# The order of Pool's work around the scan's next keys, and layer 0's norm as fused DVE operations

## The chip, the cores and the metric

The kernel runs on one core of one Trainium2 chip. A core has five engines with a queue of instructions each, worked through in order: TensorE (PE, matrix multiplies into PSUM), VectorE (DVE), ScalarE (ACT), GpSimd (POOL in the profile, Pool here) and SyncE (SP, which in this kernel issues nearly all the DMA transfers). An instruction starts when those ahead of it on its engine have started or ended and when the semaphores that it waits for have been raised by other engines or by DMA transfers. The metric is the device time of one execution in microseconds, as the median of several runs: 3565.93 us before the change (3 runs, 3565.69 to 3568.84).

## The reference, cut to what matters

The input is x of 16 batches, 512 tokens, 128 channels. Two layers follow each other, and each adds two branches to x:

```
xn = layernorm(x)
x  = x + memory(xn) + block0(xn)          # layer 0
xn = layernorm(x)
x  = x + attention1(xn) + experts1(xn)    # layer 1
```

The memory branch of layer 0 is a recurrence. The 512 tokens are cut into 8 chunks of 64; for each chunk c, the keys are k = rmsnorm(silu(xn wk)) * k_norm and the values v = silu(xn wv); a two-layer network with weights w0, w1 and a gain ln is trained by one gradient step on (k, v) of all 16 batches, the gradient is clipped by its norm, and momentum and decay give the next weights. Chunk c+1 needs the weights of chunk c. After chunk 7 the trained network is read out with queries for all tokens.

block0 is a convolution, an attention with 16 heads of 8 channels over 512 tokens, a residual, a layer norm with gain g and shift b, and eight experts of width 512 that all tokens go through, weighted by a softmax gate:

```
x  = conv(xn)
x  = layernorm(x + attention(x) @ wo.T + bo, g1, b1)     # "the norm behind layer 0's attention"
x  = layernorm(x + sum_e probs[e] * (relu(x @ w1[e] + b1[e]) @ w2[e] + b2[e]), g2, b2)
```

Layer 1 has two causal attentions with a convolution between them, and 32 experts of which each token goes to 8.

## The kernel before, in words

Everything is cut by batch into [128 partitions, 4 token tiles, 128 channels]. Each piece of work is a Python generator that writes a few instructions and then yields. A driver (`Turns.run`, line 284) goes through all live generators once per turn in the order of their priorities; a turn is one row of heads of attention scores, so that every turn holds some attention, some expert matmuls and a share of whatever else is live. `idle(n)` lets n turns pass; `room()` waits in turns for a free PSUM bank; `mark` and `after` pass word from one generator to another in turns. There are 1275 turns.

Only PE keeps the order in which the generators wrote its instructions (`manual_schedule(engines=ORDERED)`, lines 651 and 691). For DVE, ACT, Pool and SP a scheduler places each instruction on its engine's queue: by its own reckoning of when the operands are ready, and among those that are ready by the order of writing, with `high_priority` ones ahead. So a yield moves PE's instructions by a turn, and those of the other engines only as far as the scheduler lets it.

What is live in layer 0, by stage:

- Attention of batch b, every 32 turns: `front0` projects q, k, v; `tops` and `largest` (line 379) compute scores on PE and their row maximum on DVE (L404, `nm<-s`); `weighted` computes the scores again the other way round, ACT takes the exponential (L476), PE multiplies with the values; `post0` (line 1131) finishes the batch.
- `post0`: output projection on PE (`po`), bias on DVE (L1148), then `layernorm` (line 230): `moments` gives mean and variance by DVE (L222, L223) and 1/sqrt(variance + eps) by two small Pool operations (`rsqrt`, L213 and L214). Then four Pool operations normalise a token tile each (L237), one Pool operation over 128x512 multiplies by the gain (L243) and one adds the shift (L245). Four idle turns later SP stores x1 (L1153), PE transposes it, and SP stores the transposed copy (L1157). There are 16 `post0`.
- `ffn` (line 547): the eight experts of a batch, in pieces that fill the turns; after each expert Pool adds its output to a sum (L619, `ac<-ac,y`).
- `scan` (line 786): steps c = 0 to 7, 42 turns each. In a step, `hidden` computes the network's hidden layer and its slope (Pool: L891, L892), `gradient(0)` and `gradient(1)` the gradient of the output for half the tokens each. Each starts with a copy and four squares with row sums on ACT (L914, L266), the `rsqrt` of them on Pool (`r_y`), and then a multiply on DVE (L920) that waits for it. At the end of a step the clip factor `cl` goes from PE to ACT to two Pool operations (L1004, L1005) to DVE (L1007), and DVE updates the weights (L1010 to L1015).
- `project(c + 2)` is started at the end of step c: it projects keys and values of the chunk after next, squares the keys on ACT (eight L266 `sq<-k`), takes their `rsqrt` on Pool (`r_k`) and then does three Pool operations over 128x1024 each: `k<-k,sb_rowsA` (L836), `k<-k,r_k` (L838), `v<-k,v` (L840). They are called the key operations below.
- `readout` (line 1024), every six turns after the scan, 16 times: a query's projection, `rsqrt` and two Pool operations (L1034, L1035), the hidden layer (`ppq` on PE, L1047 and L1048 on ACT, L1050 on DVE into `hTq`), the output (`pyq` on PE, which reads `hTq`), `rsqrt`, one DVE operation (L1065), three Pool operations (L1066 to L1068) and a store by SP (L1070).

Layer 1 begins in turns while layer 0's last batches are still at work; it is the same before and after the change, apart from where the scheduler and the pace of the experts put its pieces.

Of the kernel before, what the change touches and what calls it, by code (L numbers as in the profile page):

```python
# [14 lines left out]
ALU = mybir.AluOpType  # L15
# [5 lines left out]
TB = S // P  # L21
# [52 lines left out]
def bc(ap, axis, n):  # L74

    u = ap.unsqueeze(axis)
    shape = list(u.shape)
    shape[axis] = n
    return u.to_broadcast(shape)
# [3 lines left out]
def network(ctx: ExitStack, tc: tile.TileContext, a, out):  # L83
    nc = tc.nc
# [30 lines left out]
    def load_rows(pool, name, names):  # L115
        t = pool.tile([P, len(names) * D], F32, bufs=1, name="sb_" + name)
        nc.sync.dma_start(t, a[name].partition_broadcast(P))
        return {n: t[:, i * D : (i + 1) * D] for i, n in enumerate(names)}
# [15 lines left out]
    row = load_rows(const, "rowsC", ["gb"])  # L134
# [28 lines left out]
    def room():  # L163

        while held[0] >= pools["work"]:
            yield
# [16 lines left out]
    def flat(ap):  # L183
        return ap.rearrange("p t d -> p (t d)")
# [24 lines left out]
    def rsqrt(dst, src, scale, eps, n):  # L209

        with tc.high_priority():
            t = sm.tile([P, n], F32, tag="rs_t", name="rs_t")
            nc.gpsimd.tensor_scalar(t, src, scale, eps, ALU.mult, ALU.add)  # L213
            nc.gpsimd.tensor_tensor(dst, t, nhalf[:, :n], ALU.pow)  # L214

    def moments(src, out):

        st = sm.tile([P, TB, 6], F32, tag="ln_st", name="ln_st")
        mv = sm.tile([P, TB, 2], F32, tag="ln_mv", name="ln_mv")
        rs = sm.tile([P, TB], F32, tag="ln_rs", name="ln_rs")  # L220
        for t in range(TB):
            nc.vector.bn_stats(st[:, t, :], src[:, t, :])  # L222
            nc.vector.bn_aggr(mv[:, t, :], st[:, t, :])  # L223
            if t == 1:
                yield
        rsqrt(rs, mv[:, :, 1], 1.0, 1e-5, TB)
        out.append((mv, rs))
        yield

    def layernorm(dst, src, gain=None, shift=None, on=None):  # L230


        got = []
        yield from moments(src, got)
        mv, rs = got[0]
        for t in range(TB):
            (on or (nc.gpsimd,))[t % len(on or (0,))].tensor_scalar(  # L237
                dst[:, t, :], src[:, t, :], mv[:, t, 0:1], rs[:, t : t + 1], ALU.subtract, ALU.mult
            )
            if t % 2 == 1:  # L240
                yield
        if gain is not None:
            nc.gpsimd.tensor_tensor(dst, dst, bc(gain, 1, TB), ALU.mult)  # L243
            yield
            nc.gpsimd.tensor_tensor(dst, dst, bc(shift, 1, TB), ALU.add)  # L245
            yield
# [26 lines left out]
    def idle(n):  # L273
        for _ in range(n):
            yield
# [493 lines left out]
    def side(*parts):  # L769

        going, parts = [], list(parts)
        while parts or going:
            if parts:
                going.append(parts.pop(0))
            going = [g for g in going if next(g, StopIteration) is not StopIteration]
            yield
# [9 lines left out]
    def scan(s1):  # L786
# [13 lines left out]
        def tokens_of(c):  # L800
            xc = s1.tile([P, B, CHUNK], F32, tag="gy", name="xc")
            nc.sync.dma_start(xc, xt[0].rearrange("b p (c t) -> c p b t", t=CHUNK)[c])
            return xc.rearrange("p b t -> p (b t)")
# [13 lines left out]
        def project(c):  # L817

            xc = tokens_of(c)
            yield from idle(3)  # L820
            k = s1.tile([P, NT, D], F32, tag="k", bufs=2, name="k")
            v = s1.tile([P, NT, D], F32, tag="v", bufs=2, name="v")

            def half(dst, w, q):
                return silu_half(
                    flat(dst[:, 4 * q : 4 * q + 4, :]),
                    lambda t: xc[:, (4 * q + t) * P : (4 * q + t + 1) * P], A(w),
                )

            yield from side(half(k, "wk", 0), half(k, "wk", 1), half(v, "wv", 0), half(v, "wv", 1))  # L830
            ks[c] = k, v
            mark("read", c)
            rk = sm.tile([P, NT], F32, tag="r_k", name="r_k")
            rms_rows(rk, k, NT, s1)
            yield
            nc.gpsimd.tensor_tensor(k, k, bc(row["kn"], 1, NT), ALU.mult)  # L836
            yield
            nc.gpsimd.tensor_tensor(k, k, bc(rk, 2, D), ALU.mult)  # L838
            yield
            nc.gpsimd.tensor_tensor(v, k, v, ALU.subtract)  # L840
            yield from idle(2)
            mark("keys", c)
# [181 lines left out]
        def readout(b):  # L1024
            xb = s1.tile([P, TB, D], F32, tag=("k", "v")[b % 2], bufs=2, name="xb")
            nc.sync.dma_start(xb, x_b[b])
            xT = s1.tile([P, S], F32, tag=("hT0", "kT")[b % 2], name="xTr")
            nc.sync.dma_start(xT, xt[0, b])
            yield from idle(2)
            q = s1.tile([P, TB, D], F32, tag=("yh", "eb", "gy", "hT1")[b % 4], name="rq")  # L1030
            yield from silu_half(flat(q), lambda t: xT[:, t * P : (t + 1) * P], A("wq"))
            rq = sm.tile([P, TB], F32, tag="r_q", name="r_q")
            rms_rows(rq, q, TB, s1)
            nc.gpsimd.tensor_tensor(q, q, bc(row["qn"], 1, TB), ALU.mult)  # L1034
            nc.gpsimd.tensor_tensor(q, q, bc(rq, 2, D), ALU.mult)  # L1035
            yield from idle(5)
            yield from room()
            qT = s1.tile([P, S], F32, tag="sg", bufs=2, name="qT")
            transpose_tokens(qT, q)
            yield from idle(1)  # L1040
            hT = s1.tile([P, 2, S], F32, tag=("h", "ds")[b % 2], name="hTq")

            def hidden(i):
                yield from room()
                pp = hold("ppq")
                mm(pp, w0T[:, i * P : (i + 1) * P], qT)
                nc.scalar.activation(hT[:, i, :], pp, AF.Tanh, scale=0.5)  # L1047
                nc.scalar.activation(hT[:, i, :], hT[:, i, :], AF.Copy, scale=0.5, bias=0.5)  # L1048
                yield
                nc.vector.tensor_tensor(hT[:, i, :], hT[:, i, :], pp, ALU.mult)  # L1050
                drop()
                yield

            yield from side(hidden(0), hidden(1))
            yield from room()
            py = toks(work("pyq"))
            for t in range(TB):
                for i in range(2):
                    mm(py[:, t, :], hT[:, i, t * P : (t + 1) * P], w1T[:, i, :], start=(i == 0), stop=(i == 1))
            ry = sm.tile([P, TB], F32, tag="r_yq", name="r_yq")  # L1060
            y = s1.tile([P, TB, D], F32, tag=("h", "ds")[b % 2], name="yq")
            nc.scalar.copy(y, py)
            rms_rows(ry, y, TB, s1)
            yield from idle(3)
            nc.vector.tensor_tensor(y, y, bc(ry, 2, D), ALU.mult)  # L1065
            nc.gpsimd.tensor_tensor(y, y, bc(ln, 1, TB), ALU.mult)  # L1066
            nc.gpsimd.tensor_tensor(y, y, q, ALU.add)
            nc.gpsimd.tensor_tensor(y, y, xb, ALU.add)  # L1068
            yield from idle(3)
            nc.sync.dma_start(acc_b[b], y)  # L1070
            yield
# [59 lines left out]
    def post0(b):  # L1131
        yield from after(("back", 0, b, 0, 0), ("back", 0, b, 0, 1))
        z = live.pop((0, b))
        xcT, cn = z["xcT"], z["cn"]
        free_values.append(z["vp"])
        yield from room()
        cT = fa.tile([P, S], F32, tag="st", bufs=2, name="cT")
        transpose_tokens(cT, cn)
        yield from idle(2)
        yield from room()  # L1140
        po = toks(hold("po"))
        for t in range(TB):
            tk = slice(t * P, (t + 1) * P)
            mm(po[:, t, :], cT[:, tk], Wt("wo"), stop=False)
            mm(po[:, t, :], xcT[:, tk], ident, start=False)
        x1 = fa.tile([P, TB, D], F32, tag="x1", bufs=1, name="x1")
        yield
        nc.vector.tensor_tensor(x1, po, bc(row["bo0"], 1, TB), ALU.add)  # L1148
        drop()
        yield  # L1150
        yield from layernorm(x1, x1, row["g1"], row["b1n"])
        yield from idle(4)
        nc.sync.dma_start(x1d[0, b], flat(x1))  # L1153
        yield from room()
        x1T = fa.tile([P, S], F32, tag="st", bufs=2, name="x1T")
        transpose_tokens(x1T, x1)
        nc.sync.dma_start(x1d[1, b], x1T)  # L1157
        mark("x1", b)
        yield
# [494 lines left out]
```

## Time and profile before

| | before |
|---|---|
| median of the runs | 3565.93 us (3565.69 to 3568.84) |
| the profiled execution's own time | 3557.66 us |
| its span, first to last instruction | 3555.9 us |
| PE busy | 3379.7 us, 95% |
| DVE busy | 2315.6 us, 65% |
| ACT busy | 2233.4 us, 63% |
| Pool busy | 1508.2 us, 42% |
| mean granted TensorE clock | 0.975 |

The profiled execution is 8.3 us, or 0.23%, faster than the median of the runs. By stage, from the table of windows: the scan's steps lie between about 130 and 1140 us, the readouts between 1140 and 1500 us, the last three `post0` of layer 0 end at about 1700 us, and what follows is layer 1 alone.

| window, us | PE idle, us | DVE busy | Pool busy |
|---|---|---|---|
| 130 to 1140 | 36.3 | 66% | 35% |
| 1140 to 1500 | 14.7 | 60% | 49% |
| 1500 to 1700 | 6.0 | 60% | 35% |
| 1700 to 3556 | 85.4 | 67% | 46% |

How to read such a table: PE works in a fixed order and is busy nearly all the time, so the time is PE's work and the gaps in it. Idle time of another engine costs nothing in itself; it counts where an instruction of PE ends up waiting for it. A second thing to read is the granted clock: after some gaps the clock stands at half for a few microseconds, and PE's work takes longer there.

### The profile page before, as it was taken

Reading aid. Unit: us, or ns where it says so; the run is one execution under the profiler, and the core shown is the slowest. Engines: PE = TensorE matmul, PEld = TensorE weight load, DVE = VectorE, ACT = ScalarE, POOL = GpSimd, SP = SyncE. Lnnn points to the kernel's source line nnn. Section 1 sums busy time; section 2 is a strip of 40 time slices with the busy share of each in tenths; the row PEclk is TensorE's granted clock in tenths of the full one; section 3 lists DMA queues with packets and bytes.
Section 4 is the critical chain, followed back from the end, with each engine's and each line's share of the span. In section 5 each row is a group of like instructions: output and inputs, shape, how many; then the busy total and the mean of one; then the engine's idle time right before and its main releaser. Section 6 shows DMA issues by size and latency. Waiting matters only on the chain.

```text
span 3555.9 us, 63951 instructions
## 1 busy us (share of the span) xinstructions
PE 3379.7 (95%) x22085; PEld 1897.3 (53%) x22085; DVE 2315.6 (65%) x6045; ACT 2233.4 (63%) x4951; POOL 1508.2 (42%) x2354
## 2 busy tenths in 40 slices
PE   6999999999999999999999999999999999998887
PEld 3445555554555555455555565555555555554443
DVE  5676666656766566556467667666666666567875
ACT  1566766775766787666656666665666666664444
POOL 5323432432431455432544344443444344433654
PEclk7999999999999999999999999999999999998998
DMA  5222222222122332443434443444344443433343
GB/s 178 70 71 77 71 82 74 74 77 83 56 85 86 102 109 87 133 122 102 135 108 122 124 125 115 130 126 121 107 122 122 124 125 98 134 106 98 93 102 93
DMA packets 289794, 370.37 MB, mean 104 GB/s; under 512 B 45984, under 2 KB 141376, under 8 KB 289088
## 3 DMA queue, kind: packets, MB, share of 16 engines
q1 hardware_dynamic: 282304, 359.46, 35.0%
q0 software_dynamic: 7168, 6.82, 1.2%
q8 instruction: 177, 2.90, 0.3%
q14 instruction: 145, 1.19, 0.1%
HBM read 236.58 MB, written 132.99 MB: 104 GB/s over the span
## 4 chain that ended last, share of the span: by engine, by line
PE 50%; DVE 5%; DMA 3%; ACT 1%; POOL 1%; issue 1%; SPq 1%; POOLq 0%; DVEq 0%; ACTq 0%
PE s L197 13%; PE pye L611 10%; PE phe L197 10%; PE pc L197 9%; PE pq L197 1%; DVE s L396 1%; PE fill L206 1%; DVE nm L404 1%; PE tpc L252 1%; PE tp L252 1%; DVE s L403 1%; PE po L197 1%; ACT e L476 1%; DMA rq<-lo 1%; PE pv L197 1%
## 5 line engine op out<-in xcount | busy, mean ns | idle before, releaser
L476 ACT ACTIVATE e<-s 128x512 f32<-128x512 f32 (+1 forms) x2432 | 1278.3, 577 | 556.4 <-PE s L197 517.2
L404 DVE TENSOR_REDUCE nm<-s 128x1 f32<-128x512 f32 (+2 forms) x1408 | 907.5, 682 | 510.1 <-PE s L197 509.2
L396 DVE CUSTOM_DVE_ANT_0 s<-s,sb_const 128x512 f32<-128x512 f32 (+1 forms) x1024 | 623.4, 643 | 390.3 <-PE s L197 388.9
L484 POOL TENSOR_SCALAR_AFFINE_SELECT e<-e 128x128 f32<-128x128 f32 (+2 forms) x1270 | 429.6, 347 | 751.0 <-ACT e L476 726.5
L197 PE MATMUL s<-kx,qx 64*128 64x512 f32 (+3 forms) x3072 | 620.4, 429 | 26.8 <-DMA kx<-rk 13.5
L197 PE MATMUL pc<-e,vp 128*32 128x512 f32 (+3 forms) x6144 | 621.7, 502 | 13.9 <-POOL e L484 7.8
L611 PEld LDWEIGHTS pye<-ew,hTe 128*128 128x128 f32 x4096 | 519.0, 192 | 178.7 <-issue 157.9
L197 PEld LDWEIGHTS s<-kx,qx 64*128 64x128 f32 x3072 | 271.2, 187 | 555.2 <-issue 219.4
L611 PE MATMUL pye<-ew,hTe 128*128 128x128 f32 x4096 | 562.3, 281 | 1.5 <-ACT hTe L601 1.4
L197 PE MATMUL s<-qx,kx 64*128 64x512 f32 (+3 forms) x3072 | 535.7, 356 | 27.2 <-DVE nm L404 8.4
L197 PE MATMUL phe<-x1T,ew 128*128 128x512 f32 x1024 | 551.1, 623 | 7.8 <-DMA ew<-in_ew 3.1
L601 ACT ACTIVATE hTe<-phe,sb_cols 128x512 f32<-128x512 f32 x512 | 354.1, 692 | 245.2 <-PE phe L197 242.8
L197 PEld LDWEIGHTS s<-qx,kx 64*128 64x128 f32 x3072 | 305.5, 188 | 80.4 <-ACT e L476 19.1
L619 POOL TENSOR_TENSOR ac<-ac,y 128x512 f32<-128x512 f32 x128 | 163.9, 1280 | 425.9 <-ACT y L618 363.9
L403 DVE TENSOR_TENSOR s<-s,sb_const 128x256 f32<-128x256 f32 (+1 forms) x384 | 181.6, 515 | 190.5 <-PE s L197 157.4
L197 PEld LDWEIGHTS pc<-e,vp 128*32 128x32 f32 x6144 | 151.4, 110 | 238.1 <-issue 173.2
L197 PEld LDWEIGHTS phe<-x1T,ew 128*128 128x128 f32 x1024 | 158.8, 193 | 75.0 <-issue 44.1
L618 ACT ACTIVATE y<-pye,pr 128x128 f32<-128x128 f32 x512 | 147.5, 370 | 30.6 <-PE pye L611 26.2
L396 DVE DVE_READ_ACCUMULATOR2_ANT nm<- 128x1 f32 x1024 | 144.1, 141 | 0.0
L213 POOL TENSOR_SCALAR rs_t<-ss 128x4 f32<-128x4 f32 (+1 forms) x56 | 12.0, 215 | 221.5 <-ACT sq L266 220.0
L1470 POOL DMA_INDIRECT acc<-eo,sidx x32 | 52.0, 1624 | 72.2 <-DVE eo L1464 26.3
L213 POOL TENSOR_SCALAR rs_t<-ln_mv 128x4 f32<-128x4 f32 x64 | 12.8, 200 | 162.3 <-DVE ln_mv L223 159.4
(302 smaller groups left out, 3906.4 us busy)
## 6 DMA issues: line engine op xcount, KB each, us to landing
ew<-in_ew SPq DMA_DIRECT2D x256, 256.0 KB
kx<-rk SPq DMA_DIRECT2D x192, 256.0 KB
qx<-rq SPq DMA_DIRECT2D x128, 256.0 KB
rq<-hi SPq DMA_DIRECT2D x64, 256.0 KB
rq<-lo SPq DMA_DIRECT2D x64, 256.0 KB
rk<-hi SPq DMA_DIRECT2D x64, 256.0 KB
rk<-lo SPq DMA_DIRECT2D x64, 256.0 KB
qx<-r SPq DMA_DIRECT2D x64, 256.0 KB
```

The source lines that it names most:

```text
L197: nc.tensor.matmul(o, lhsT=lhsT, rhs=rhs, start=start, stop=stop)
L252: nc.tensor.transpose(tp[:, t * P : (t + 1) * P], src(t), ident)
L396: newest[0] = nc.vector.tensor_tensor_reduce(out=sv[r][:, 0, :], in0=sv[r][:, 0, :], in1=row["caus"][:, S - n :], scale=1.0, scalar=-BIG, ...
L403: nc.vector.tensor_tensor(dg, dg, bc(row["caus"][:, S - P :], 1, per), ALU.add)
L404: newest[0] = nc.vector.tensor_reduce(nm[:, qt, r, t : t + per], sv[r], AX.X, ALU.max)
L476: nc.scalar.activation(e[:, r, 0 : per * n], s[r], AF.Exp, scale=SCALE)
L484: cleared[0] = nc.gpsimd.affine_select(out=ev[:, r, :, 0:P], in_=ev[:, r, :, 0:P], pattern=[[0, per], [1, P]], compare_op=ALU.is_ge, fill= ...
L601: nc.scalar.activation(hs[i], ph, AF.Relu, bias=col("fb", i))
L611: nc.tensor.matmul(pye[0][:, t, :], lhsT=h[:, t * P : (t + 1) * P], rhs=w2[e][:, f, :], start=(f == 0 and t == 0), stop=(f == 3), skip_gro ...
L618: nc.scalar.mul(y[:, t, :], pye[0][:, t, :], pr[:, t, e : e + 1])
L619: nc.gpsimd.tensor_tensor(ac, ac, y, ALU.add)
L1470: nc.gpsimd.indirect_dma_start(out=acc, out_offset=bass.IndirectOffsetOnAxis(ap=sidx[:, e : e + 1], axis=0), in_=eo[:, i, :], in_offset=No ...
```

## The change

Three places are edited.

- In `project`, one yield between the squares of the keys and the key operations becomes nine idle turns, except for chunks 0 and 1.
- In `readout`, one more idle turn stands between the hidden layer and the output's matmuls `pyq`.
- In `post0`, the call of `layernorm` is replaced: `moments` stays, with its small Pool `rsqrt`; then four DVE operations compute (x - mean) * gain for a token tile each, and four more compute that times 1/sqrt(variance + eps), plus the shift. Two are written per turn. The wait before the store is two turns in place of four.

```diff
@@ project(c)
             rms_rows(rk, k, NT, s1)
-            yield
+            yield from idle(9 if c > 1 else 1)
             nc.gpsimd.tensor_tensor(k, k, bc(row["kn"], 1, NT), ALU.mult)
             yield
             nc.gpsimd.tensor_tensor(k, k, bc(rk, 2, D), ALU.mult)
@@ readout(b)
             yield from side(hidden(0), hidden(1))
+            yield from idle(1)
             yield from room()
             py = toks(work("pyq"))
@@ post0(b)
-        yield from layernorm(x1, x1, row["g1"], row["b1n"])
-        yield from idle(4)
+        got = []
+        yield from moments(x1, got)
+        mv, rs = got[0]
+        for t in range(TB):
+            nc.vector.scalar_tensor_tensor(
+                x1[:, t, :], x1[:, t, :], mv[:, t, 0:1], row["g1"], ALU.subtract, ALU.mult
+            )
+            if t % 2 == 1:
+                yield
+        for t in range(TB):
+            nc.vector.scalar_tensor_tensor(
+                x1[:, t, :], x1[:, t, :], rs[:, t : t + 1], row["b1n"], ALU.mult, ALU.add
+            )
+            if t % 2 == 1:
+                yield
+        yield from idle(2)
         nc.sync.dma_start(x1d[0, b], flat(x1))
```

The two new groups of DVE operations are at lines 1156 and 1162 of the changed kernel; lines behind them are 15 higher than before.

## The prediction

> **What bounds the kernel now.** I read the page first: PE is busy 95% of the span. Then the table of windows by stage. The change lies between 130 and 1580 us, and there PE is idle 51.6 us, of which 36.3 fall in the scan's steps and 14.7 in the readouts (columns: window, length, PE busy, weight loads, DVE, ACT, Pool, granted clock, DMA):
>
> ```profile
> 130.00:1140.00 1010.00, 973.66 (x5713) 537.50 (x5705) 666.22 (x1226) 680.18 (x1558) 354.96 (x335) 0.99 0.26 74
> 1140.00:1500.00 360.00, 345.35 (x2036) 183.90 (x2035) 215.52 (x384) 275.53 (x712) 177.77 (x183) 0.99 0.36 107
> ```
>
> So nothing but a gap of PE can be won, and half clock behind a gap. Third, the waits from 130 to 1600 us (total, times, longest): PE waits most for the row maxima of DVE, and DVE in turn for two small Pool results.
>
> ```profile
> PE s L197 <- DVE nm L404: 15.5, 14, 4.2
> ...
> DVE yh L920 <- POOL r_y L214: 23.5, 6, 9.9
> ...
> DVE cl L1007 <- POOL cl L1005: 4.5, 1, 4.5
> ```
>
> Fourth, the timelines of these places. At the end of scan step 3, the norm behind the attention stands on Pool ahead of the clip factor; DVE stands at L1007 with the maxima behind it, and PE stops:
>
> ```profile
> 622.05 3.15 POOL L237 TENSOR_SCALAR x<-x,ln_mv,ln_rs 128x128 f32<-128x128 f32 x4
> ...
> 626.39 1.28 POOL L243 TENSOR_TENSOR x<-x,sb_rows 128x512 f32<-128x512 f32 x1
> 627.75 1.26 POOL L245 TENSOR_TENSOR x<-x,sb_rows 128x512 f32<-128x512 f32 x1
> ...
> 629.89 0.16 DVE L1007 RECIPROCAL cl<-cl 128x1 f32<-128x1 f32 x1 [4.47 <-POOL cl L1005]
> ...
> 631.95 0.49 PE L197 MATMUL s<-kx,qx 64*128 64x512 f32 x1 [3.34 <-DVE nm L404]
> ```
>
> In step 5 the key operations of the next chunk stand on Pool ahead of the second gradient's `r_y`:
>
> ```profile
> 792.88 2.73 POOL L836 TENSOR_TENSOR k<-k,sb_rowsA 128x1024 f32<-128x1024 f32 x1
> ...
> 799.25 2.34 POOL L840 TENSOR_TENSOR v<-k,v 128x1024 f32<-128x1024 f32 x1
> ...
> 801.96 1.01 POOL L214 TENSOR_TENSOR r_y<-rs_t,nhalf 128x4 f32<-128x4 f32 x1
> ...
> 803.00 0.69 DVE L920 TENSOR_TENSOR yh<-yh,r_y 128x512 f32<-128x512 f32 x1 [6.28 <-POOL r_y L214]
> ...
> 804.34 0.79 PE L197 MATMUL s<-kx,qx 64*128 64x512 f32 x2 [4.23 <-DVE nm L404]
> ```
>
> And three gaps in the readouts, with the clock behind the second and third (eighth column):
>
> ```profile
> 1228.39 1.13 PE L197 MATMUL ppq<-qT,sb_pa 128*128 128x512 f32 x2 [2.02 <-ACT hTe L601]
> ...
> 1343.51 2.80 PE L197 MATMUL pyq<-sb_pa,hTq 128*128 128x128 f32 x11 [3.05 <-DVE hTq L1050]
> ...
> 1425.09 1.65 PE L197 MATMUL pgt<-sb_gw,x1T 128*128 128x8 f32 x8 [1.70 <-DMA x1T<-x1d]
> ...
> 1343.00:1347.00 4.00, 3.49 (x17) 3.48 (x18) 0.96 (x2) 0.65 (x2) 0.00 (x0) 0.57 0.50 151
> 1425.00:1433.00 8.00, 7.91 (x32) 3.44 (x34) 2.36 (x6) 3.53 (x12) 1.01 (x1) 0.57 0.77 220
> ```
>
> A clock of 0.57 over 4 us is 0.43 x 4 = 1.7 us of PE work lost; over 8 us it is 3.4. The window from 633 to 637 us shows 0.57 too.
>
> **The nine turns.** They do nothing. Built with this edit alone, the program has on all five engines the instruction order of the kernel before. The scheduler places Pool's work by when operands are ready, and the key operations follow their squares. In the changed kernel they still stand between the first and the second `r_y` in steps 2, 3, 5 and 6. Price 0, and the 6.28 us stall of step 5 stays.
>
> **The norm taken off Pool.** Each of 16 `post0` loses six Pool operations: 3.15 + 1.28 + 1.26 = 5.7 us, 91 us in all. Pool is not the bound, so I count only the places where something waits behind them.
>
> (a) Step 3's clip factor. In the new Pool order only the norm's `rsqrt` (done at 621.94) and one L619 (1.27 us) precede it, its operand is there at 622.3, and the pair takes 0.9 us: done at about 624.2 against 629.9, before DVE asks in earnest. The gap of 3.34 and the 1.7 of clock go: -5.0.
>
> (b) The gap at 1425. SP stood at the store L1153 from 1404 to 1414 us for L245, then at the readout's store L1070 until 1421.6 for Pool operations that had queued behind the norm; the load of x1T came after both. Without the norm (6.2 us there) and with the readout one turn later (six turns are 18.9 us, so 3.15) the load is issued 3 us earlier, more than the 1.70 that PE waited. -1.7 - 3.4 = -5.1.
>
> (c) The gap at 1228 and 0.66 us at 1218.8 (PE waits for `rq` of L1035). Both follow a norm on Pool, 1208.6 to 1215.0: L1034 and L1068 come behind it, and ACT's L1047, which starts at 1226.5, writes the buffer that readout 1's store, issued only at 1223.96, still reads. 6.4 us earlier and one turn later is 3.2 earlier, more than the 2.02: -2.7.
>
> **The readout's idle turn.** At 1343 `pyq` followed `hTq` at once; a turn of 3.15 us just covers 3.05: -3.05 - 1.7 = -4.75. The cost: the store of one readout comes a turn nearer to the write of the buffer by the readout after next. The tightest pairs apart from (c) lie 5.9 and 6.2 us apart from issue to write, and a store takes some 2.5 us; 3.15 more fits. 0.
>
> **What the change puts in the way.** (d) In step 4 the key operations ran before both `r_y` (650.98 to 660.51 us) and nobody waited. In the new Pool order they stand between the two, as in the other steps. There the second `r_y` ends 14.4 to 15.6 us after the first; in step 4 that is 682.0 to 683.2, and DVE comes to its multiply at 677.47: a new stall of 4.5 to 5.7 us. What PE pays for such a stall the four other steps show: 9.90 us of stall cost 1.1 (gap at 436.8), 3.63 cost 2.7 (546.7 to 555.4), 1.18 cost 5.0 (929.6 to 945.1 with one half-clock stretch), 6.28 cost 12.6 (gaps of 4.23, 1.15, 1.38 and 0.69, clock 1.7 + 3.4). The mean is 5.4; less 0.4 that step 4 lost already, +5.0, with ends 0.7 and 12.2.
>
> (e) In steps 2 and 5 an L619 now stands between the sum of squares and the second `r_y`: 1.27 us on top of both stalls. Ends 0 (step 2's 9.90 hardly cost anything) and 2.5 (once for once): +2.5, since step 5 passed most of its stall on.
>
> (f) DVE gets 128 operations. The nearest row is L1011, the same kind at 128x128: it starts at 630.95 and the next at 631.21, so 0.26 us each, 33 us. Each reads two SBUF operands, and such operations are stretched while Pool works: L1065 has a mean of 975 ns against 679 undisturbed, the eight groups of 16 from L920 to L942 average 744 against some 675. I take 0.1 us each, 13 us. These 46 us go into DVE's idle time (344 us in the scan's window), but four groups stand among the maxima, and the second pair waits for Pool's `rsqrt`, with the maxima of that turn queued behind it and PE behind those. Ends: 0, and all 46 on PE. From 130 to 1580 us DVE is busy 927 us, 622 of them in L404; the other 305 cost PE the 15.5 us of waits for L404, 5%. By that rate 46 us cost +2.3.
>
> [...]
>
> SP's two stores of x1 come two turns earlier; what waited behind L1153 on SP waited 87 us over ten times, and only (b) reached PE. The work left on PE is the same but for 512 columns of filler.
>
> **The sum.** (a) to (c) and the readout's turn: -5.0 - 5.1 - 2.7 - 4.75 = -17.55; with (d) to (f) -17.55 + 5.0 + 2.5 + 2.3 = -7.75. The profiled execution would go from 3557.66 to 3549.9; it lies 8.3 below the median of the runs, so the median goes from 3565.9 to 3558.
>
> **Rivals.** First, nothing measurable: step 4 pays like step 5, 12.2 in place of 5.0, and the sum is -0.6: 3565.3. For it: the same engines and the same pattern; against it: two of the four steps paid under 3. Second, slower: DVE becomes what PE waits for. The place is the four groups in front of L404 in each `post0`; from 17 of their 46 us on PE, 15 more than my 2.3, the change is slower by 7; at half, 23, the sum is +13: 3579. For it: 14 waits for L404 already, and DVE two thirds busy; against it: most DVE idle time before L404 (477 us) is spent waiting for PE. Third, more gain: step 4 pays as little as step 2, 0.7, and the sum is -12.1: 3553.9. Fourth, the nine turns do after all what they say: then the 1.1 + 2.7 + 12.6 + 5.0 = 21.4 of the four steps go, with (d) and (e): -17.55 - 21.4 + 2.3 = -36.7: 3529. The instruction order speaks against it.
>
> **Numbers.** About 0.2%, 7.1 us, is what a measurement of this kernel can tell from no change. Forecast 0.33, third rival 0.10, fourth 0.02: faster 0.45. First rival, and cases between: same 0.31. Second: slower 0.24. The forecast's own range is 3551 to 3559. The whole range reaches down to (d) and (f) at their low ends with some gap more (3546), up to near the second rival (3577).
>
> **What would show it.** Right: no gap of 3 us before 632; no SP wait for Pool at L1153; `pyq` without a wait for `hTq`; a new DVE wait for `r_y` in step 4 of about 5 us, and those of steps 2, 3 and 5 still there. Wrong: key operations behind the second `r_y`; PE's wait for L404 far above 15 us in the window to 1600; new gaps in layer 1, where the pieces of the experts shift and 91 us of PE idle time after 1500 could move either way.

## The result, and the profile after

The changed kernel is slower: 3576.13 us in the median of 13 runs against 3565.69 us in 13 runs of the kernel before on the same chip, a ratio of 1.0024 with a 95% interval of 1.0014 to 1.0034, or some 9 us. The prediction had said 3558, and faster.

The profiled execution of the changed kernel took 3576.36 us, at its median. That of the kernel before took 3557.66, some 8 us below its own. So the two profiles lie 18.7 us apart, of which some 10 are only the difference between two executions. The first experiment below has the instruction order of the kernel before on all five engines and was profiled at 3563.34 us; it serves as a second profile of that order.

The table of windows by stage of the changed kernel (columns as in the prediction):

```profile
130.00:1140.00 1010.00, 964.58 (x5657) 536.22 (x5653) 682.19 (x1291) 672.37 (x1542) 294.49 (x273) 0.99 0.26 74
1140.00:1500.00 360.00, 351.45 (x2063) 185.56 (x2064) 229.02 (x412) 274.65 (x725) 162.89 (x167) 1.00 0.37 109
1500.00:1700.00 200.00, 189.73 (x1145) 104.71 (x1144) 120.30 (x339) 120.79 (x248) 47.85 (x63) 0.96 0.37 106
```

PE is idle 45.4 us in the scan's steps, where it was 36.3; 8.5 in the readouts, where it was 14.7; and 10.3 from 1500 to 1700 us, where it was 6.0 and where nothing was expected. Two lines of the table of waits from 130 to 1600 us say the same of the scan (the first was 23.5 before, the second 15.5; the line for the clip factor is gone):

```profile
DVE yh L920 <- POOL r_y L214: 28.2, 7, 8.8
...
PE s L197 <- DVE nm L404: 21.1, 14, 6.8
```

The timeline of the changed kernel at the clip factor of step 3, at the stalls for the second `r_y` in steps 3, 4 and 5 (with what stands ahead of `r_y` on Pool in steps 4 and 5), at two places of the readouts, and at 1590 us:

```profile
553.25 0.69 DVE L920 TENSOR_TENSOR yh<-yh,r_y 128x512 f32<-128x512 f32 x1 [3.60 <-POOL r_y L214]
...
554.60 0.79 PE L197 MATMUL s<-kx,qx 64*128 64x512 f32 x1 [4.17 <-DVE nm L404]
...
630.45 0.61 POOL L1004 TENSOR_TENSOR cl<-cl,phalf 128x1 f32<-128x1 f32 x1
...
633.53 0.15 DVE L1007 RECIPROCAL cl<-cl 128x1 f32<-128x1 f32 x1
...
680.33 2.84 POOL L840 TENSOR_TENSOR v<-k,v 128x1024 f32<-128x1024 f32 x1
...
684.57 0.69 DVE L920 TENSOR_TENSOR yh<-yh,r_y 128x512 f32<-128x512 f32 x1 [3.62 <-POOL r_y L214]
...
685.91 0.65 PE L197 MATMUL s<-qx,kx 64*128 64x512 f32 x1 [3.95 <-DVE nm L404]
...
810.85 1.26 POOL L619 TENSOR_TENSOR ac<-ac,y 128x512 f32<-128x512 f32 x1
...
813.12 0.69 DVE L920 TENSOR_TENSOR yh<-yh,r_y 128x512 f32<-128x512 f32 x1 [8.51 <-POOL r_y L214]
...
814.47 0.80 PE L197 MATMUL s<-kx,qx 64*128 64x512 f32 x2 [6.84 <-DVE nm L404]
...
1232.35 1.12 PE L197 MATMUL ppq<-qT,sb_pa 128*128 128x512 f32 x2 [0.82 <-ACT qT L259]
...
1355.79 2.05 PE L197 MATMUL pyq<-sb_pa,hTq 128*128 128x128 f32 x16
...
1590.84 3.55 PE L197 MATMUL phe<-x1T,ew 128*128 128x512 f32 x4 [3.90 <-issue]
```

The stall of step 3 in the kernel before:

```profile
551.81 0.69 DVE L920 TENSOR_TENSOR yh<-yh,r_y 128x512 f32<-128x512 f32 x1 [3.63 <-POOL r_y L214]
...
553.16 1.13 PE L197 MATMUL phe<-x1T,ew 128*128 128x512 f32 x2 [1.23 <-DVE nm L404]
```

All four gaps that the change was to close are closed: the clip factor no longer waits, nor does `pyq`; the wait at `ppq` is down to 0.82 us, and the one for x1T at 1425 us is gone. Step 4 has the new stall that was foretold, step 5 a longer one. But step 3 costs more with the same stall: DVE waits 3.60 us, as it did before (3.63), and PE now stops for 4.17 us where it had stopped for 1.23, with 6.8 us of half clock from 553.0 us on, where in the profile of before there was none. And one gap lies where nothing had been looked for, at 1590 us: PE waits 3.90 us for the first expert matmuls of a batch.

To compare whole executions, I cut each trace at the first, tenth and fourteenth of DVE's bias operations of `post0`, and 5 us behind the sixteenth. Each cell is the length of the stage in us and, in brackets, PE's idle time plus half the length of the half-clock stretches in it (where the two overlap, both count).

| kernel | scan | readouts | the next 190 us | rest of the span |
|---|---|---|---|---|
| order of before (e1) | 892.0 (42.4) | 388.7 (20.0) | 192.4 (9.9) | 1871.3 |
| changed | 900.1 (51.6) | 382.5 (10.2) | 200.6 (18.8) | 1874.3 |

The scan gave 8 us away, the readouts brought 6, and the third stage, where nothing had been expected, cost 8 more. The 3.0 us of the rest are less than two executions of one order differ by there, as is shown further below.

### The profile page after: what moved, and what is told of

Same layout as the page of the kernel before. It is cut to its first block, busy times and chain, and to the rows that moved or that the text cites. A ratio compares the mean times of both kernels' runs of the same rounds, so it can differ in the third digit from the quotient of the medians.

```text
span 3574.6 us, 63940 instructions
## 1 busy us (share of the span) xinstructions
PE 3390.9 (95%) x22083; PEld 1906.2 (53%) x22083; DVE 2361.1 (66%) x6173; ACT 2228.1 (62%) x4951; POOL 1410.9 (39%) x2258
## 4 chain that ended last, share of the span: by engine, by line
PE 80%; DVE 8%; ACT 4%; DMA 3%; POOL 3%; issue 2%; SPq 1%; POOLq 0%; DVEq 0%; ACTq 0%
PE s L197 20%; PE pc L197 13%; PE pye L611 13%; PE phe L197 13%; DVE nm L404 3%; PE tp L252 2%; PE pgr L197 2%; PE fill L206 1%; ACT e L476 1%; PE tpc L252 1%; PE pq L197 1%; PE po L197 1%; PE pj L197 1%; DVE s L396 1%; PE pcv L197 1%
## 5 line engine op out<-in xcount | busy, mean ns | idle before, releaser
L404 DVE TENSOR_REDUCE nm<-s 128x1 f32<-128x512 f32 (+2 forms) x1408 | 907.5, 682 | 486.5 <-PE s L197 485.5
L197 PE MATMUL s<-qx,kx 64*128 64x512 f32 (+3 forms) x3072 | 544.2, 357 | 28.8 <-DVE nm L404 8.9
L619 POOL TENSOR_TENSOR ac<-ac,y 128x512 f32<-128x512 f32 x128 | 164.1, 1282 | 447.8 <-ACT y L618 420.2
```

The costliest lines, as they stand in the source:

```text
L197: nc.tensor.matmul(o, lhsT=lhsT, rhs=rhs, start=start, stop=stop)
L404: newest[0] = nc.vector.tensor_reduce(nm[:, qt, r, t : t + per], sv[r], AX.X, ALU.max)
L619: nc.gpsimd.tensor_tensor(ac, ac, y, ALU.add)
```

## The experiments

Every ratio is to the kernel before, on the same chip in the same session. The labels are numbered in the order of the runs. In a variant's timeline the line numbers are shifted by the lines that its edit adds (L406 is L404 in e5, L1071 is L1070 in e2).

**e1: the nine turns alone.** The kernel before with the first edit of the change and nothing else.

```diff
             rms_rows(rk, k, NT, s1)
-            yield
+            yield from idle(9 if c > 1 else 1)
```

> The kernel before with the nine turns alone. If they do nothing, as the instruction order says: a ratio of 1.000, within 0.1% of the kernel before, and the stall of DVE for the second r_y in step 5 stays at about 6 us. If they act as named, the four steps' stalls go: about 20 us faster, 3545.

1.0000 (0.9988 to 1.0012); the stall in step 5 is 6.28 us, to the hundredth that of the kernel before. The first part of the change does nothing, as predicted.

**e2: the readout's turn alone.**

```diff
             yield from side(hidden(0), hidden(1))
+            yield from idle(1)
             yield from room()
```

> The kernel before with the readout's idle turn alone. By the prediction's term, the gap of 3.05 us and the half clock behind it go at 1343 us: -4.75, a ratio of 0.9987, with the scan's steps as before. Rival: the pieces of the experts that shift by a turn open a gap elsewhere (after 1500 us), and the ratio is 1.000 or above.

1.0039 (1.0022 to 1.0055): 14 us slower, the rival's ratio. `pyq` no longer waits at 1343 us. A gap of 3.37 us opens in layer 1, at 2237 us, as the rival had it (more under e10), but a longer one lies a little ahead of the old place:

```profile
1318.93 1.27 POOL L1069 TENSOR_TENSOR yq<-yq,xb 128x512 f32<-128x512 f32 x1
1320.23 0.37 SPq L1071 DMA_DIRECT2D acc<-yq  x1
...
1322.76 0.60 ACT L1047 ACTIVATE hTq<-ppq 128x512 f32<-128x512 f32 x1 [5.38 <-DMA acc<-yq]
...
1324.99 0.80 PE L197 MATMUL s<-qx,kx 64*128 64x512 f32 x2 [5.14 <-DVE hTq L1050]
```

This is the cost that the prediction had named and put at 0: the store of one readout (L1071 here) has come a turn nearer to ACT's write of the same buffer by the readout after next. With the norm still on Pool the three operations before the store queue up behind it, and ACT waits 5.38 us for the store.

**e3: the norm on DVE alone**, with the change's two idle turns, without the nine turns and the readout's turn.

```diff
-        yield from layernorm(x1, x1, row["g1"], row["b1n"])
-        yield from idle(4)
+        got = []
+        yield from moments(x1, got)
...
+        yield from idle(2)
         nc.sync.dma_start(x1d[0, b], flat(x1))
```

> The kernel before with the norm on DVE alone (neither nine turns nor the readout's turn). First theory (the loss of the change lies in the scan, by the stalls for r_y that this part moves and by what PE has written behind them): the scan's steps end about 9 us later, gaps of 4 us in steps 3 and 4 as in the changed kernel; with the gaps at 1425 and 1228 gone in part, a ratio of 1.002 to 1.004. Second theory (DVE's 46 us more are what PE waits for): the same ratio, but gaps spread over all sixteen norms. Third theory (an accident of queue order at 1590 us costs the 5.6 us): the ratio is within 0.1% of 1.000 if the gap of 3.90 us at 1590 is not there.

1.0008 (0.9998 to 1.0018), the ratio of the third theory with the scan of the first. The scan is that of the changed kernel: gaps of 4.17, 3.95 and 6.85 us in steps 3, 4 and 5. The gaps at 1228 and 1425 us are gone without the readout's turn, and there is none at 1590.

**e4: the changed kernel with the key operations behind the second `r_y`**, by an order that the scheduler must keep (`small[0]` is the last instruction of `rsqrt`).

```diff
@@ gradient(q), behind rms_rows
+                if q == 1:
+                    second[0] = small[0]
+                    mark("second", c)
@@ project(c), behind rms_rows
-            yield from idle(9 if c > 1 else 1)
-            nc.gpsimd.tensor_tensor(k, k, bc(row["kn"], 1, NT), ALU.mult)
+            if c > 1:
+                yield from after(("second", c - 1), lag=1)
...
+                behind.enter_context(tc.issue_after(second[0].ins))
+                nc.gpsimd.tensor_tensor(k, k, bc(row["kn"], 1, NT), ALU.mult)
```

> The changed kernel with the key operations put on Pool's queue behind the second r_y by a forced order (in place of the nine turns). First theory: DVE no longer waits for the second r_y, and of the 34 us that PE loses in steps 2 to 6 in gaps behind those stalls and half clock (2.7, 7.6, 5.7, 13.4, 5.2) the most goes: 3545 to 3560, a ratio to the kernel before of 0.994 to 0.998. Second theory (DVE's load): the gaps move to other waits for the row maxima, 3572 to 3578. Third theory (1590): also 3570 or more, with the gap of 3.90 us there still.

0.9997 (0.9985 to 1.0008), some 10 us less than the changed kernel by the ratios, and short of what the first theory expected. The gaps in steps 3, 4 and 5 fall to 1.12, 0.52 and 1.00 us. Those of 1.3 and 1.1 us behind 817 us and one of 3.02 in step 6 stay: they had not been due to the stalls. The gap at 1590 is there, with 4.89 us.

**e5: the same forced order in the kernel before.** Edit as in e4, without the rest of the change.

> The kernel before with the key operations forced behind the second r_y, the norm still on Pool. First theory (the scan's loss in the changed kernel was all by those stalls): the stalls of 9.9, 3.6 and 6.3 us in steps 2, 3 and 5 go, and with them about 2 us of PE in step 2, 1 in step 3 and 4.2 with 1.7 of clock in step 5: 6 to 9 us faster, 0.9975 to 0.9985; the gaps of 1.2 to 1.4 us behind 817 us stay, as they did in the changed kernel so treated. If DVE's 46 us had cost something in that kernel's scan, this one ends its steps earlier than that one by more than the 3.3 that the gap in step 3 still costs here. Rival (other Pool work queued behind the key operations comes late instead): 1.000 or more.

1.0002 (0.9991 to 1.0013): a miss. The gap of 4.2 us in step 5 is gone, but step 2 has a new one of 3.29 with 6.8 us of half clock. The timeline of this kernel shows Pool catching up there and DVE slowed beside it:

```profile
434.69 1.28 POOL L247 TENSOR_TENSOR x<-x,sb_rows 128x512 f32<-128x512 f32 x1
434.73 1.80 DVE L952 TENSOR_TENSOR gt<-yh,m 128x512 f32<-128x512 f32 x1
435.93 1.50 POOL L946 TENSOR_TENSOR gy<-gy,th 128x512 f32<-128x512 f32 x1
436.44 1.53 DVE L944 TENSOR_TENSOR gt<-gy,sb_rowsA 128x512 f32<-128x512 f32 x1
...
440.30 0.79 PE L197 MATMUL s<-qx,kx 64*128 64x512 f32 x1 [3.29 <-DVE nm L406]
```

DVE operations that take 0.68 us undisturbed (the last of them, L953 here, is L942 before: 0.67 to 0.69 us, 16 times) take 1.5 to 1.8 while Pool's stand beside them. The stall was moved, not removed.

**e6: norm on DVE with two turns, and the key operations behind**, without the readout's turn.

> The norm on DVE and the key operations behind the second r_y, without the readout's turn and the nine turns. First theory with the readout's turn as a loss: the norm's 1.0008 less the 9.8 us that the forced order was worth: 0.998, some 7 us faster than before, no gap at 1590 us, one of about 3.5 at 1350. Rival (the forced order's gain depends on the readout's turn): 1.000.

0.9978 (0.9969 to 0.9987), as expected, and faster than both kernels. No gap at 1590 us.

**e7: DVE's load by itself.** The norm stays on Pool; beside it 128 fused operations run on DVE whose results nothing reads. The norm's Pool operations stand in the same loop and are not shown.

```diff
+        for t in range(2 * TB):
+            nc.vector.scalar_tensor_tensor(
+                cT[:, (t % TB) * P : (t % TB + 1) * P], row["g1"], (mv[:, t, 0:1] if t < TB else rs[:, t - TB : t - TB + 1]), row["b1n"], ALU.mult, ALU.add
+            )
...
```

> The kernel before with the norm left on Pool, and at the places where the changed kernel has its 128 fused DVE operations 128 of the same kind whose results nothing reads (they write a transposed buffer that is done with). This is the price of DVE's load alone. The prediction's term: +2.3 us, a ratio of 1.0006. Second theory: 8 to 23 us, 1.002 to 1.006. If the load is free: 1.000.

1.0012 (1.0002 to 1.0023): 4.3 us, between 0.7 and 8.2. The prediction's 2.3 lies inside, the second rival's 17 and more do not. The price is rather high than low: with the norm still on Pool beside them, these 128 operations last 70 us in all, those of the changed kernel 62. The timeline shows how it costs at its worst place, in step 2:

```profile
430.45 2.48 DVE L1155 SCALAR_TENSOR_TENSOR cT<-sb_rows,ln_rs 128x128 f32<-128x128 f32 x2
430.47 1.26 POOL L619 TENSOR_TENSOR ac<-ac,y 128x512 f32<-128x512 f32 x1
...
432.86 1.28 DVE L404 TENSOR_REDUCE nm<-s 128x1 f32<-128x512 f32 x2
433.68 0.66 PE L252 MATMUL tpc<-sb_const,cs 128*128 128x128 f32 x2 [4.68 <-DVE nm L404]
```

**e8: the readout's turn with the output in a buffer of its own.**

```diff
-            xb = s1.tile([P, TB, D], F32, tag=("k", "v")[b % 2], bufs=2, name="xb")
+            xy = s1.tile([P, NT, D], F32, tag=("k", "v")[b % 2], bufs=2, name="xb")
+            xb = xy[:, 0:TB, :]
...
-            y = s1.tile([P, TB, D], F32, tag=("h", "ds")[b % 2], name="yq")
+            y = xy[:, TB:NT, :]
```

> The readout's turn on the kernel before, with the readout's output in a buffer of its own (the spare half of that of xb), so that ACT's write of hTq two readouts later no longer waits for the store. If that wait is what cost the readout's turn alone its gap of 5.14 us at 1325 and the half clock of 6.8 us behind it: both are gone and the ratio falls from 1.0039 to about 1.0015. If the gap's cause is another, it stays and so does 1.004.

0.9994 (0.9981 to 1.0006). The gap at 1325 us and its half clock are gone, so the store was its cause. In the stage of the readouts this kernel takes 379.9 us, against 391.2 in e2 and 388.7 in e1. The 9 us that it wins there do not appear in the ratio: in layer 1, between the same two marks (the first `pq` of two batches, 2149 and 2269 us here), it takes 119.8 us where e1 takes 112.4.

**e9: the norm on DVE with the four idle turns kept.** One number differs from e3.

```diff
-        yield from idle(2)
+        yield from idle(4)
         nc.sync.dma_start(x1d[0, b], flat(x1))
```

> The norm on DVE, with the four idle turns before the store kept as in the kernel before; PE's instruction order is then that of the kernel before, and the key operations of step 4 stay ahead of both r_y. Theory A (not the DVE operations but the two turns taken from this wait cost the scan its 8 us: the experts of a batch start two turns sooner, other pieces stand on PE behind each stall, and the Pool work moves with them): step 3's gap is 1.2 us and not 4.2, step 4 has none, step 5 has 4.2 and not 6.8, and the gaps at 632, 1228 and 1425 us are gone; with 4 us for DVE's load a ratio of 0.9965 to 0.9980. Theory B (DVE's operations themselves): the scan ends 8 us late as in the changed kernel, 1.001.

0.9944 (0.9926 to 0.9962): 20 us faster than before, the best of all and more than either theory expected. Its timeline at the stall of step 3, where e3 and the changed kernel lose 4.17 us:

```profile
548.25 0.40 PE L197 MATMUL s<-qx,kx 64*128 64x512 f32 x2
548.58 1.16 PE L611 MATMUL pye<-ew,hTe 128*128 128x128 f32 x8
549.57 1.02 PE L197 MATMUL phe<-x1T,ew 128*128 128x512 f32 x2
550.43 1.05 PE L611 MATMUL pye<-ew,hTe 128*128 128x128 f32 x8
551.36 0.69 DVE L920 TENSOR_TENSOR yh<-yh,r_y 128x512 f32<-128x512 f32 x1 [3.62 <-POOL r_y L214]
552.71 1.12 PE L197 MATMUL phe<-x1T,ew 128*128 128x512 f32 x2 [1.22 <-DVE nm L404]
```

Three groups of expert matmuls stand between the scores and the place where PE waits, and they cover most of DVE's stall of 3.62 us. In the changed kernel, with a stall of 3.60, the next thing in PE's order is another row of scores, and the experts come behind it:

```profile
549.95 0.49 PE L197 MATMUL s<-kx,qx 64*128 64x512 f32 x1
...
554.61 1.38 PE L197 MATMUL s<-qx,kx 64*128 64x512 f32 x2
...
555.92 2.07 PE L611 MATMUL pye<-ew,hTe 128*128 128x128 f32 x8
```

**e10: the changed kernel with four idle turns**, all else as it is (the edit of e9 on the changed kernel).

> The changed kernel with one number put back: four idle turns before the store of x1 in place of two. Theory A: the slowdown of 1.0024 is all in these two turns: 0.996 to 0.998, with the gap of 3 us at 1343 gone too and no gap of 3.9 at 1590. Theory B: 1.002.

0.9982 (0.9970 to 0.9994). One number put back turns 1.0024 into a gain of 6 us. Against e9 it has the readout's turn more (the nine turns do nothing), and that costs it 14 us by the ratios. Its gap at 1343 us is gone all the same; what comes instead is in layer 1, at 2218 us:

```profile
2211.86 0.50 SPq L339 DMA_DIRECT2D rq<-hi  x1
...
2217.27 0.69 ACT L333 ACTIVATE hi<-pjk,sb_cols 128x512 fp32r<-128x512 f32 x1 [3.38 <-DMA rq<-hi]
...
2218.59 0.79 PE L197 MATMUL s<-qx,kx 64*128 64x512 f32 x1 [3.01 <-ACT hTe L601]
```

ACT waits for a store out of a buffer that it must overwrite, and PE behind ACT. In e2 and e8, which have the same PE order, ACT waits 3.74 and 2.96 us at this place and PE 3.37 and 2.59; in e9 ACT waits 0.46 and PE not at all.

**e11: the key operations of step 4 between the two `r_y`**, in the kernel before, by a forced order behind the first `r_y`.

> The kernel before with one thing moved: in step 4 the key operations are forced behind the first r_y, and so stand between the two as in the other steps. The prediction's term for this was +5.0 us, with ends of 0.7 and 12.2: a ratio of 1.0014, a stall of DVE of 4.5 to 5.7 us and a gap of PE behind it of about 4 us with half a clock of 1.7. If PE has expert work between the scores there, which hides the stall: 1.000 and no gap.

0.9997 (0.9982 to 1.0013), one gap of 0.74 us. The squares of the keys were long done, so the key operations began right behind the first `r_y`, at 671.25 us; the second `r_y` was done at 679.76, and DVE came to it at 682.78 without a wait. So they were done before DVE came, and no stall arose: their place between the two costs nothing by itself.

**e12: the load of x1T ahead of the row loads**, in the changed kernel, for the gap at 1590 us.

```diff
-        nc.sync.dma_start(x1T, x1d[1, b])
+        with tc.high_priority():
+            nc.sync.dma_start(x1T, x1d[1, b])
```

> The changed kernel with the load of x1T given priority on SP, so that at 1583 us it stands ahead of nine of the ten row loads of 256 KB behind which it stood. If that place on SP is what cost the gap of 3.90 us at 1590 and the half clock of 6.8 us around it, 7 us go: 1.0004. If the row loads then come late in its place (the gaps at 1663 grow), it stays at 1.0024.

1.0025 (1.0011 to 1.0038), although the gap is gone. Here the load is issued at 1577.21 us, and the stage takes 192.0 us instead of 200.6. The timeline of SP in the changed kernel shows where it had stood, behind the row loads of an attention (eight of 256 KB, `qx<-rq` and `kx<-rk`, two of them shown; the two more that the expectation counts, `qx<-zrow`, have 16 KB):

```profile
1578.28 0.43 SPq L373 DMA_DIRECT2D qx<-rq  x1
...
1579.97 0.42 SPq L373 DMA_DIRECT2D kx<-rk  x1
...
1583.21 0.34 SPq L542 DMA_DIRECT2D x1T<-x1d  x1
```

What was won is lost again in layer 1: e12 has a new gap of 3.51 us at 2023.92 us, where PE waits for `qx<-top`, with 10.2 us of half clock beside it, and between the first `pq` of the two batches around it (1924 and 2044 us) it takes 119.9 us where the changed kernel takes 112.4.

**e13: the two turns alone.** The norm stays on Pool; the wait before the store is two turns. PE's order is then that of e3.

> The kernel before with the norm left on Pool and two idle turns in place of four before the store of x1: PE's instruction order is then that of the norm on DVE with two turns (e3). If the two turns alone make the loss: with four turns the norm on DVE gave 0.9944, with two 1.0008, so 0.0064 or 23 us slower than before, 1.004 to 1.008, with gaps of 4.2, 4.0 and 6.8 us in steps 3, 4 and 5. If they cost only together with DVE's operations: 1.000 to 1.002.

1.0044 (1.0029 to 1.0060), 16 us. Without one operation more on DVE, its timeline has the three gaps of the changed kernel:

```profile
553.50 0.79 PE L197 MATMUL s<-kx,qx 64*128 64x512 f32 x1 [4.17 <-DVE nm L404]
...
691.57 0.79 PE L197 MATMUL s<-qx,kx 64*128 64x512 f32 x1 [3.96 <-DVE nm L404]
...
820.93 0.79 PE L197 MATMUL s<-kx,qx 64*128 64x512 f32 x2 [6.84 <-DVE nm L404]
```

**e14 and e15: six and three turns**, with the norm on DVE.

> The norm on DVE with six idle turns before the store. If sooner is worse (the loads and the experts of a batch collide with more): 0.994 or less. If any other place of the experts' pieces than the one that the kernel before was tuned to costs something: above 0.9944, between 0.997 and 1.003; the key operations of step 4 stand between the two r_y here too.

> The norm on DVE with three idle turns before the store; in step 4 the key operations are ahead of both r_y, and no further L619 stands before the second r_y in steps 2 and 5. If Pool's order makes the loss: like four turns, 0.994 to 0.996. If the place of the pieces on PE makes it: between 0.996 and 1.002, wherever a stall meets no expert matmuls.

Six turns: 0.9973 (0.9962 to 0.9985), gaps of 3.03, 1.36 and 3.96 us in steps 3, 4 and 5. Three turns: 0.9966 (0.9951 to 0.9980), 1.23, none and 4.20. So sooner is not simply worse: two turns are the worst of the four, four the best, and the two others lie between, though the intervals of three and four turns overlap. For three turns the interval reaches into what both theories expected; it does not tell them apart.

**e16: e9 with the key operations behind the second `r_y`.**

> The norm on DVE with four turns, and the key operations behind the second r_y by a forced order. If the gaps of PE behind the stalls that are left there are lost time (4.2 us and half clock in step 5, 1.3 and 1.2 in steps 2 and 3): 6 to 8 us off 0.9944, 0.992. If, as with the kernel before (1.0002), other Pool work that stands behind the key operations gives it back: 0.994 to 0.996.

0.9954 (0.9937 to 0.9970). The gap of 4.20 us in step 5 goes, that of 1.22 in step 3 becomes one of 1.50, and nothing is won, as in e5.

The ratios in one table:

| | readout as before | with the readout's turn |
|---|---|---|
| norm on Pool, four turns | 1 | 1.0039 (e2) |
| norm on Pool, two turns | 1.0044 (e13) | not run |
| norm on DVE, four turns | 0.9944 (e9) | 0.9982 (e10) |
| norm on DVE, two turns | 1.0008 (e3) | 1.0024 (the change) |

From 1 by way of e9 and e3 to the change: the norm on DVE -20 us, the two turns +23, the readout's turn +6. Four chips were used (e1 to e4, e5 to e8, e9 to e12, e13 to e16), and a difference of two ratios carries both intervals: 23 us is 23 give or take some 7, and the three prices of the readout's turn, 14 (e2), 14 (e10 against e9) and 6, lie within 5 to 8 us of error each. And the stages of some of these kernels, as in the table above:

| kernel | scan | readouts | the next 190 us | rest of the span |
|---|---|---|---|---|
| e13 | 909.2 (60.7) | 396.1 (28.2) | 190.0 (8.7) | 1879.7 |
| e3 | 899.9 (51.5) | 381.7 (12.9) | 191.7 (10.1) | 1876.0 |
| e9 | 886.7 (37.9) | 383.9 (15.2) | 192.2 (10.2) | 1860.1 |
| e10 | 887.4 (38.1) | 382.6 (10.5) | 190.8 (7.4) | 1870.7 |

## Why the prediction was wrong

**The step that failed** stands in two sentences at the end of the costs: "SP's two stores of x1 come two turns earlier; what waited behind L1153 on SP waited 87 us over ten times, and only (b) reached PE. The work left on PE is the same but for 512 columns of filler." The two turns taken from the wait before the store were priced at 0, by looking at what they do to SP. What they do is start the experts of each batch two turns sooner, since `ffn` waits for the mark that `post0` sets behind its store, and with that they shift the expert matmuls in PE's order, and Pool's order with them. Measured: 16 us alone (e13), 23 us from e9 to e3, 15 from e10 to the change.

Where the sum missed, the losses in brackets tell, e1 against the changed kernel. The scan lost 9.2 us more, where (a) and (d) to (f) make 4.8; the readouts lost 9.8 less, where (b), (c) and the readout's turn make 12.6; the third stage lost 8.9 more, where the sum had nothing. That is 16 us in this pair of profiles, about what lies between the -7.75 of the sum and the 9 measured. What the sum had at nothing in the scan is step 3, 2.9 us of gap and 3.4 of half clock; the effects of the two turns in steps 4 and 5 it held under (d) and (e). In the profiles of e9 and e3, 13 us of the price of the two turns lie in the scan and 16 behind 1700 us; those 16 are half clock (44.6 and 63.0 us lost there), and no run shows what brings it.

**What shows the mechanism.** In step 3 DVE's stall is the same, 3.60 to 3.63 us, in every kernel with two to four turns and no forced order. It costs 1.2 us where expert matmuls stand behind the scores and 4.17 where they do not: here it is PE's order that the two turns change. In steps 4 and 5 it is the stall: 3.62 us where there was none and 8.51 in place of 6.28, behind the key operations and an L619 on Pool. How the whole price divides between the two orders is not shown; e15, which was to tell them apart, does not. The prediction took PE's price for a stall from four places of one kernel, as if it belonged to the stall. It belongs to the neighbours in PE's order, and the change moved these. The reading was off in two of the four places as well: the gaps of 1.15 and 1.38 us behind 817 us, and most of what step 6 loses, stay where the stall is gone (e4, e5).

**(a) to (c), the norm off Pool: right, and by the ratio worth more than the sum gave.** All three gaps go, with the readout's turn, which the working had counted against (b) and (c), and in e9 without it. With the load (f) in it, the norm on DVE brings 20 us, where the terms (a) to (c) and (f) make 10.5. In the profiles of e9 and e1, 5.3 of these lie in the scan and 4.8 in the readouts. The rest, 11 us behind 1700 us, where both have the same PE order, is not settled: 12 of it are half clock in the last 350 us, and two executions with the order of before differ there by 10.5 (39.6 and 50.1 us lost). It is not one profile's accident alone: the six runs of e9 have a mean granted clock of 0.9765, the 29 runs of the kernel before in that session 0.9719, and by this 17 of the 21 us between their means are lost clock.

**The readout's turn: wrong in sign.** The gap of 3.05 us at 1343 goes, as predicted. The cost through the buffer, put at 0, is 0 only with the norm off Pool; on the kernel before it is the gap of 5.14 at 1325 (e2, e8). And like the two turns it changes PE's order: in e10 a gap in layer 1 takes the gain back. In the changed kernel the gap at 1590 comes with both edits (e3 and e10, with one each, do not have it), but closing it wins nothing (e12). The term was -4.75; the ratios say +14 (e2), +14 (e10 against e9) and +6 (the change against e3).

**(d) and (e): the sizes nearly right, by luck.** Step 4 cost 3.95 us and 1.7 of clock in the changed kernel against +5.0 predicted, the L619 in step 5 2.6 us and 1.7 against +2.5. The key operations in between do make these stalls: forced behind the second `r_y`, they give back some 10 us in the changed kernel (e4). But both come with the two turns, which were priced at 0, with the norm still on Pool (e13), and neither comes with the norm on DVE and four turns (e9). The same place between the two `r_y`, made alone, cost nothing (e11).

**(f): right in kind, low by half, and inside the interval.** 4.3 us (0.7 to 8.2) against 2.3. In the trace of the changed kernel the shortest of the 128 operations lasts 0.32 us, and the 58 that have no Pool operation beside them at most 0.35. The ten longest last 1.35 to 1.8 us, and each of them ends some 0.15 us behind the end of a Pool operation of 1.28 to 2.4 us beside it: the longest, 1.82 us from 415.53, behind an L836 that ends at 417.20. The durations of the 128 add up to 62 us, where 128 times the shortest would be 40: they were held up by some 21 us, where the prediction took 13. DVE's busy time in all grows by 45 us from e1 to the changed kernel (2316.4 to 2361.1), close to the 46 of the prediction.

**The nine turns:** price 0, and 1.0000 measured (e1).

**The rivals.** Slower was the second rival's side, but not by its mechanism: DVE's load is well below the 17 us from which it would have decided. None of the rivals had the order of the experts in it; that their pieces shift stood only in the last line, among what would make the prediction wrong, without a price.

## What to carry to other kernels

Where generators are interleaved turn by turn, a delay of a turn or two is an edit of the order of everything that follows: build the variant with the old delay as well, and read what the bottleneck engine has queued behind each known stall, before and after. A stall of another engine has no price of its own; it costs what the bottleneck cannot cover from its own queue at that place (here DVE's stall of 3.6 us in step 3 cost PE 1.2 us or 4.17). And an idea that came out slower may be a good one in bad company: here one number, four for two, made 0.9944 of 1.0008.

## What the runs showed of the hardware

The half clock (a granted clock of 0.50) came in stretches of 3.41 us and multiples of it: in the kernel before 3.41 us from 633.41 and from 804.08, 6.83 from 824.56 and from 1425.30; in the changed kernel 6.83 from 552.99, 3.41 from 1590.64 and from 1597.46, 10.24 from 1662.32. PE's work took twice as long in it: eleven of the `pyq` at 1343.51 us took 2.80 us before, 0.25 each; the sixteen at 1355.79 us in the changed kernel, at full clock, took 2.05, 0.13 each. Whether a short gap brought half clock differed from execution to execution. The gap of 1.2 us behind DVE's stall in step 3 is the same in the kernel before, e1, e9, e2 and e11 (1.21 to 1.23); the first three have no half clock there (a granted clock of 1.00 from 553 to 560 us in the kernel before), the other two 6.8 us of it (0.67 and 0.66 over the same 7 us). The window of e2 shows it, and below it the same window of the kernel before (eighth column, the granted clock):

```profile
553.00:560.00 7.00, 6.28 (x16) 1.58 (x16) 5.45 (x10) 2.08 (x4) 2.63 (x2) 0.67 0.11 37
...
553.00:560.00 7.00, 6.35 (x29) 2.72 (x30) 6.93 (x13) 3.68 (x7) 3.35 (x3) 1.00 0.10 37
```

That is worth 3.4 us in one execution, as much as many of the terms above. So half clock followed a gap of 1.2 us in two of the five.

A longer such stretch near 3265 us, in layer 1's last phase, is 23.9 us long in fourteen of the eighteen profiles of this study (in the kernel before from 3265.09 us) and 41.0 in four (in the changed kernel from 3273.41), 8.5 us of lost time apart; e11 and the kernel before have the same PE order, and one of each.
